# Moving small per-query work from VectorE to GpSimd and ScalarE in a differential-attention and mixture-of-experts kernel

## The chip, the cores and the metric

One NeuronCore of a Trainium2 chip runs the whole kernel. The metric is the device time of one execution in microseconds (us); the figure given for a kernel is the median of several runs. A profile is one further execution, recorded by the hardware profiler. The engines are TensorE (PE; its weight loads are PEld), VectorE (DVE), ScalarE (ACT), GpSimd (POOL) and SyncE (SP), which here only starts transfers.

## The reference

`x` is 8 x 512 x 128 in float32; there are 16 heads of width 8 and 8 experts with a hidden width of 512. Two layers follow each other, each with a residual and a layer norm:

```python
def attn(x, Wq, Wk1, Wk2, Wv, Wo, lambda_logit):
    q, k1, k2, v = heads(x @ Wq.T), heads(x @ Wk1.T), heads(x @ Wk2.T), heads(x @ Wv.T)
    a1 = softmax(causal(q @ k1.T * SCALE)); a2 = softmax(causal(q @ k2.T * SCALE))
    a = a1 - sigmoid(lambda_logit) * a2
    a = a / maximum(sum(abs(a)), 1e-6)
    return merge(a @ v) @ Wo.T

def ffn(x, gamma, beta, router_w, W1, W2):
    xn = layernorm(x) * gamma + beta
    p = softmax(xn @ router_w.T / 1.5)
    w, idx = top_k(p, 2)
    y_e = silu(xn @ W1[e]) @ W2[e]
    return sum_over_e(dense(w, idx)[e] * y_e) + x

x = layernorm(x + attn(x)); x = layernorm(x + ffn(x))
```

## The kernel before

**Attention.** For each of the 8 batches the 512 queries are cut into 16 strips of 32. A strip `j` with its keys is one `Unit`; it sees `L = 32 (j + 1)` keys. The 16 heads are 4 groups (`g`) of 4 heads, so one group's scores for a strip are 128 rows (4 heads x 32 queries) by `L` columns. A unit with `L` up to 256 ("early") is done in two slots, a longer one ("late") in four; a slot makes the scores of two groups (early: both softmaxes at once; late: one of the two). That makes 48 slots a batch and 384 in all.

Per slot: PE writes scores into one of two PSUM tiles `sc` (L327, L336); DVE takes the negated row maxima `nm` (L349, L357); ACT takes the exponentials into `et` and, through an accumulator that a second instruction reads, their row sums (L367). Per unit: DVE works out the ratio `c2` = sigmoid(lambda) * sum1 / sum2 in three tiny instructions (`ratios`, L379, L382, L383). Per piece of a unit (two groups when early, one when late), `combine`: DVE forms max(c2 * e2, e1) and its row sum (L393, which gives the absolute sum later on), POOL scales e2 by -c2 in place (L403) and may gather left-over columns into `rest` (L417), PE then transposes both tiles into one PSUM accumulation, which is also the subtraction (L448), ACT copies the result to `aT` (L473), and PE multiplies by the values (L490).

**Order.** Nothing is left to a scheduler. `round_of`, called once a slot, issues the instructions of all engines in the order in which they stand: values times, scores of the next slot, `aT` copies, `on_act`, maxima of this slot, transposes, `on_dve`, combining of pieces of the unit before, exponentials of this slot, `on_dve_late`, and then one step each of the filler work. Each engine works through its own list in that order, so an instruction that waits holds everything behind it on its engine.

**Filler work.** `misc` holds the small steps after a block of four strips (`block_tasks`: normalise, project out, residual and layer norm, turn `xnT`, L595, router logits) and the projections of the next batch (`projection_tasks`: `xT`, L251; `qs`, L268; `kT`, L276; `vt`, L284). `routing` holds the top-2 routing of a chunk of 6 or 9 blocks. `moves` are the indirect transfers that sort rows by expert into `xs`, `gathers` those that fetch results back (`got`, L925) for mixing (`mix`, L935) and the last layer norm (its root on POOL by a power, L90). `experts` holds the expert tiles of a chunk, 128 rows each: `load` (weights and `xg`, on SP), `turn` and `hidden`. `turn(t)` transposes `xg[t]` (L871) and, into the other half of the same PSUM tile `pa`, multiplies the tile three steps back by its second matrix (L880); `xgT` is made by DVE (L874), `ysb` by ACT (L890). `hidden(t)` multiplies by the first matrix into a PSUM tile `pz` (L900) of the same two-buffer pool; ACT takes the tanh (L845), DVE finishes the SiLU `hT` (L847). Experts are taken from their list at a pace that `times` and `go` set. The last sparse chunk (19 tiles) and one dense chunk (2 blocks) come after the last slot: in the tail there is no attention to hide behind.

## Time and profile before

| | before |
|---|---|
| median of 3 runs | 1220.2 us (1216.79 to 1223.67) |
| the profiled execution | 1212.04 us |
| span of its profile, first to last instruction | 1210.1 us |
| granted PE clock, mean | 0.927 |
| PE, DVE, ACT, POOL busy | 90%, 77%, 64%, 44% of the span |

The span is divided at the first maxima of a unit. By these, attention runs from about 19 us to 1087 us, and the tail takes the last 123 us. The costliest groups are the transposes (L448, PE, 326.7 us), the exponentials (L367, ACT, 300.4 us late and 188.6 us early), the scaling (L403, POOL, 270.9 us), the combining (L393, DVE, 258.6 us), and the maxima (L357, DVE, 252.0 us). A group's row in the profile gives its busy time, the mean of one instruction, and the idle time of its engine just before it with what ended that idle time. PE's busy time has modelled ends and can hold short stalls.

### The profile page before, as it was taken

Reading aid. Unit: us, or ns where it says so; the run is one execution under the profiler, and the core shown is the slowest. Engines: PE = TensorE matmul, PEld = TensorE weight load, DVE = VectorE, ACT = ScalarE, POOL = GpSimd, SP = SyncE. Lnnn points to the kernel's source line nnn. Section 1 sums busy time; section 2 is a strip of 40 time slices with the busy share of each in tenths; the row PEclk is TensorE's granted clock in tenths of the full one; section 3 lists DMA queues with packets and bytes.
Section 4 is the critical chain, followed back from the end, with each engine's and each line's share of the span. In section 5 each row is a group of like instructions: output and inputs, shape, how many; then the busy total and the mean of one; then the engine's idle time right before and its main releaser. Section 6 shows DMA issues by size and latency. Waiting matters only on the chain.

```text
span 1210.1 us, 28192 instructions
## 1 busy us (share of the span) xinstructions
PE 1093.9 (90%) x9450; PEld 776.2 (64%) x9450; DVE 927.1 (77%) x2837; ACT 780.4 (64%) x2775; POOL 526.8 (44%) x935
## 2 busy tenths in 40 slices
PE   5999899989999899989998999988999989997686
PEld 3566565555666566666666666666667667777675
DVE  4688778777887887987887878887767898874556
ACT  3678767576777777766766867774567566662221
POOL 4343433463423442267464432333554652444333
PEclk7699969797999999989998999997899799998998
DMA  4400000110221112100322222221213344444762
GB/s 133 122 8 1 10 2 8 31 56 30 50 63 46 54 32 67 45 27 27 93 69 58 73 54 68 64 73 31 81 52 91 95 120 124 122 123 129 207 177 67
DMA packets 128895, 84.28 MB, mean 70 GB/s; under 512 B 22896, under 2 KB 114288, under 8 KB 128752
## 3 DMA queue, kind: packets, MB, share of 16 engines
q1 hardware_dynamic: 111952, 68.26, 20.2%
q0 software_dynamic: 3840, 7.87, 2.3%
q10 hardware_dynamic: 12960, 6.36, 1.8%
q8 instruction: 75, 1.23, 0.4%
q14 instruction: 68, 0.56, 0.2%
HBM read 63.31 MB, written 17.56 MB: 67 GB/s over the span
## 4 chain that ended last, share of the span: by engine, by line
PE 60%; DVE 16%; ACT 11%; issue 6%; POOL 4%; DMA 3%; ACTq 1%; POOLq 0%; SPq 0%; DVEq 0%
PE pt L448 19%; PE sc L327 13%; ACT et L367 7%; PE po L490 5%; PE pz L900 5%; PE pa L880 5%; PE sc_None L327 5%; DVE junk L393 2%; DVE nm L357 2%; PE pmo L541 2%; ACT aT L473 2%; DVE nm L349 2%; POOL et L403 1%; DVE hT L847 1%; POOL xs L777 1%
## 5 line engine op out<-in xcount | busy, mean ns | idle before, releaser
L403 POOL TENSOR_SCALAR et<-et,c 128x224 f32<-128x224 f32 (+15 forms) x512 | 270.9, 534 | 458.1 <-DVE junk L393 295.0
L448 PE MATMUL pt<-ident,et 128*128 128x128 f32 (+1 forms) x2048 | 326.7, 296 | 26.8 <-ACT aT L473 14.9
L448 PEld LDWEIGHTS pt<-ident,et 128*128 128x128 f32 (+1 forms) x2048 | 230.5, 145 | 159.6 <-issue 58.2
L367 ACT ACTIVATE et<-sc,nm 128x512 f32<-128x512 f32 (+7 forms) x512 | 300.4, 595 | 48.7 <-DVE nm L357 27.6
L357 DVE TENSOR_REDUCE nm<-sc 128x2 f32<-128x576 f32 (+7 forms) x256 | 252.0, 984 | 45.1 <-PE sc L336 44.6
L473 ACT COPY aT<-pt 128x384 f32<-128x384 f32 (+5 forms) x488 | 186.1, 407 | 134.5 <-PE pt L448 130.7
L393 DVE SCALAR_TENSOR_TENSOR junk<-et,c 128x224 f32<-128x224 f32 (+15 forms) x512 | 258.6, 505 | 9.6
L327 PE MATMUL sc<-kT,qb 32*128 32x384 f32 (+7 forms) x1024 | 246.8, 559 | 10.9 <-ACT et L367 9.6
L367 ACT ACTIVATE et<-sc_None,nm 128x256 f32<-128x256 f32 (+7 forms) x512 | 188.6, 387 | 32.0 <-DVE nm L349 22.0
L327 PE MATMUL sc_None<-kT,qb 32*128 32x512 f32 (+7 forms) x512 | 116.5, 535 | 21.8 <-ACT et L367 21.0
L900 PE MATMUL pz<-xgT,w 128*128 128x128 f32 x704 | 102.1, 291 | 18.8 <-DVE xgT L874 18.5
L349 DVE TENSOR_REDUCE nm<-sc_None 128x4 f32<-128x256 f32 (+7 forms) x128 | 96.1, 751 | 29.6 <-PE sc_None L336 29.3
L327 PEld LDWEIGHTS sc<-kT,qb 32*128 32x128 f32 x1024 | 78.3, 187 | 61.3 <-ACT et L367 27.4
L367 ACT ACTIVATION_READ_ACCUMULATOR et<-sc_None,nm 128x1 f32 x512 | 108.1, 211 | 0.0
L900 PEld LDWEIGHTS pz<-xgT,w 128*128 128x128 f32 x704 | 92.5, 204 | 23.6 <-DVE xgT L874 21.2
L367 ACT ACTIVATION_READ_ACCUMULATOR et<-sc,nm 128x1 f32 x512 | 103.9, 203 | 0.0
L880 PE MATMUL pa<-w,hT 128*128 128x128 f32 x704 | 98.1, 285 | 0.6 <-ACT ysb L890 0.6
L845 ACT ACTIVATE th<-pz 128x512 f32<-128x512 f32 x88 | 52.7, 599 | 68.9 <-PE pz L900 47.9
L880 PEld LDWEIGHTS pa<-w,hT 128*128 128x128 f32 x704 | 90.9, 202 | 1.3 <-ACT ysb L890 0.7
L777 POOL DMA_INDIRECT xs<-xh,row x60 | 65.9, 1099 | 46.9 <-DMA xs<-xh,row 31.3
L490 PE MATMUL po<-aT,vt 128*32 128x128 f32 (+1 forms) x2048 | 85.3, 290 | 0.0
L847 DVE SCALAR_TENSOR_TENSOR hT<-th,pz 128x512 f32<-128x512 f32 x88 | 60.2, 684 | 30.8 <-ACT th L845 30.6
(150 smaller groups left out, 1281.0 us busy)
## 6 DMA issues: line engine op xcount, KB each, us to landing
w<-in_w_dram SPq DMA_DIRECT2D x192, 256.0 KB
xg<-xs SPq DMA_DIRECT2D x88, 64.0 KB
ys<-ysb ACTq DMA_DIRECT2D x88, 64.0 KB
xs<-zero SPq DMA_DIRECT2D x2, 1600.0 KB
xs<-zero SPq DMA_DIRECT2D x2, 1216.0 KB
xt<-in_x_dram SPq DMA_DIRECT2D x8, 256.0 KB
out_dram<-ot SPq DMA_DIRECT2D x32, 64.0 KB
vr<-vt SPq DMA_DIRECT2D x32, 32.0 KB
```

The source lines that it names most:

```text
L327: nc.tensor.matmul(parts[gi][:, :, :L], lhsT=qb[r, j].rearrange("p h q -> p (h q)"), rhs=kT[r, sets, :L], start=True, stop=False,)
L349: nc.vector.tensor_reduce(self.nm[:, g, :], sc.rearrange("p g (s l) -> p g s l", s=2)[:, :, :, : self.L], AX.X, ALU.max, negate=True,)
L357: nc.vector.tensor_reduce(self.nm[:, g, s], sc[:, :, : self.L], AX.X, ALU.max, negate=True)
L367: nc.scalar.activation(self.et[:, g, si, : self.L], sc[:, gi, lo : lo + self.L], AF.Exp, bias=self.nm[:, g, si : si + 1], accum_out=self.b ...
L393: nc.vector.scalar_tensor_tensor(junk[:, :L], self.et[:, g, 1, :L], self.c2[:, g : g + 1], self.et[:, g, 0, :L], ALU.mult, ALU.max, accum_ ...
L403: nc.gpsimd.tensor_scalar(self.et[:, g, 1, :L], self.et[:, g, 1, :L], self.c2[:, g : g + 1], -1.0, ALU.mult, ALU.mult,)
L448: nc.tensor.matmul(pt[: len(gs) * kw, x_, :], lhsT=lhsT, rhs=ident, is_transpose=True, start=(k == 0), stop=(k == 1),)
L473: nc.scalar.copy(self.aT[: rows[done], self.used + done : self.used + end, :], pt[: rows[done], done:end, :],)
L490: nc.tensor.matmul(self.blk["po"][32 * g : 32 * g + 32, self.jj, :], lhsT=v[:rows, kb, 32 * g : 32 * g + 32], rhs=self.aT[:rows, self.at[g ...
L777: nc.gpsimd.indirect_dma_start(ch.xs[:, :], bass.IndirectOffsetOnAxis(ap=ch.row[:, k, c : c + 1], axis=0), ch.xh[:, c, :], None,)
L880: nc.tensor.matmul(pm[:, 1, :], lhsT=hT[y][:, f, :], rhs=w[y][1][:, f, :], start=(f == 0), stop=(f == NF - 1),)
L900: nc.tensor.matmul(pz[:, f, :], lhsT=w[t][0][:, f * P : (f + 1) * P], rhs=xgT[t], start=True, stop=True,)
```

## The change

It has six parts.

1. The evacuations of `xT`, `qs`, `vt`, `xnT` and `xgT` go from DVE to ACT (the last two as an Identity activation with scale and bias).
2. `weighted`, issued at the end of a unit's last slot, makes c1 on POOL; for late units it makes the whole of `c2` there, with a power of -1 in place of the reciprocal.
3. For units with `L` up to 96, the maximum is taken over both groups of a piece in one instruction and summed by a second, from the already scaled e2, on `on_dve_late`.
4. A routing step goes ahead of `misc`; the two joined pairs of routing steps become single steps; the projections get a list of their own, behind `misc`.
5. In the tail `pz` takes its PSUM tile from the pool of the scores.
6. `w1st`, `w2nd` and `row` go to a pool with three buffers; a constant in `times` goes from 24 to 22.

The place of `run(on_dve_late)`, after combining and exponentials, is the same in both kernels.

```diff
+    mone = const.tile([P, NG], F32, name="mone")
+    nc.gpsimd.memset(mone, -1.0)
...
-                on_dve.append(lambda: nc.vector.tensor_copy(xT, pm))
+                on_act.append(lambda: nc.scalar.copy(xT, pm))
...
-                    nc.vector.tensor_copy(qs, pm)
+                    nc.scalar.copy(qs, pm)
...
-                    nc.vector.tensor_copy(vt, pm)
+                    nc.scalar.copy(vt, pm)
...
             def ratios(self):
                 sums, jj = self.blk["sums"], self.jj
-                c1 = sp.tile([P, NG], F32, tag="c1", name=f"c1_{self.b}_{self.j}")
-                nc.vector.tensor_mul(c1, sums[:, 0, jj, :], slam)
+                if self.c2 is not None:
+                    return
                 self.c2 = sp.tile([P, NG], F32, tag="c2", name=f"c2_{self.b}_{self.j}")
                 r2 = sp.tile([P, NG], F32, tag="r2", name=f"r2_{self.b}_{self.j}")
                 nc.vector.reciprocal(r2, sums[:, 1, jj, :])
-                nc.vector.tensor_mul(self.c2, c1, r2)
+                nc.vector.tensor_mul(self.c2, self.c1, r2)
+
+            def weighted(self):
+                self.c1 = sp.tile([P, NG], F32, tag="c1", name=f"c1_{self.b}_{self.j}")
+                nc.gpsimd.tensor_tensor(self.c1, self.blk["sums"][:, 0, self.jj, :], slam, ALU.mult)
+                if not self.early:
+                    self.c2 = sp.tile([P, NG], F32, tag="c2", name=f"c2_{self.b}_{self.j}")
+                    nc.gpsimd.tensor_tensor(
+                        self.c2, self.blk["sums"][:, 1, self.jj, :], mone, ALU.pow
+                    )
+                    nc.gpsimd.tensor_tensor(self.c2, self.c1, self.c2, ALU.mult)
...
-                L = self.L
-                for g in piece:
-                    nc.vector.scalar_tensor_tensor(
-                        junk[:, :L],
-                        self.et[:, g, 1, :L],
-                        self.c2[:, g : g + 1],
-                        self.et[:, g, 0, :L],
-                        ALU.mult,
-                        ALU.max,
-                        accum_out=self.blk["big"][:, self.jj, g : g + 1],
-                    )
+                L, g0, m = self.L, piece[0], len(piece)
+                small = L <= 96
+
+                def largest():
+                    first, second = (self.et[:, g0 : g0 + m, k, :L] for k in range(2))
+                    big = self.blk["big"][:, self.jj]
+                    if small:
+
+                        both = junk[:, : m * L].rearrange("p (g l) -> p g l", g=m)
+                        nc.vector.scalar_tensor_tensor(both, second, -1.0, first, ALU.mult, ALU.max)
+                        nc.vector.tensor_reduce(big[:, g0 : g0 + m], both, AX.X, ALU.add)
+                        return
+                    for k, g in enumerate(piece):
+                        nc.vector.scalar_tensor_tensor(
+                            junk[:, :L],
+                            second[:, k],
+                            self.c2[:, g : g + 1],
+                            first[:, k],
+                            ALU.mult,
+                            ALU.max,
+                            accum_out=big[:, g : g + 1],
+                        )
+
+                if not small:
+                    largest()
                 for g in piece:
                     nc.gpsimd.tensor_scalar(
...
+                if small:
+                    on_dve_late.append(largest)
...
-                on_dve.append(
-                    lambda: nc.vector.tensor_scalar(s["xnT"], pm, gam, bet, ALU.mult, ALU.add)
+                on_act.append(
+                    lambda: nc.scalar.activation(
+                        s["xnT"], pm, AF.Identity, bias=bet, scale=gam
+                    )
                 )
...
-            tasks = [largest, first, second, together(weights, chosen), counts]
-            tasks += [together(starts, rows), owners]
+            tasks = [largest, first, second, weights, chosen, counts]
+            tasks += [starts, rows, owners]
...
-                    on_dve.append(
-                        lambda: nc.vector.tensor_scalar(
-                            xgT[t], pm[:, 0, :], gam, bet, ALU.mult, ALU.add
+                    on_act.append(
+                        lambda: nc.scalar.activation(
+                            xgT[t], pm[:, 0, :], AF.Identity, bias=bet, scale=gam
                         )
                     )
...
-                pz = ps_m.tile([P, NF, P], F32, tag="pm", name=f"pz_{n0}_{t}")
+
+                pool, tag = (ps_s, "sc") if attention_done else (ps_m, "pm")
+                pz = pool.tile([P, NF, P], F32, tag=tag, name=f"pz_{n0}_{t}")
...
-                behind = seq * (24 + (2 * ch.nb + 3 if ch.sparse else 0)) / 48
+                behind = seq * (22 + (2 * ch.nb + 3 if ch.sparse else 0)) / 48
...
-            if misc:
-                misc.popleft()()
-                room -= 1
+
             if routing:
                 step = routing.popleft()
                 step()
                 room -= step.__name__ == "counts"
+            elif misc or proj:
+                (misc or proj).popleft()()
+                room -= 1
+            if now and now["left"] == 1:
+                now["u"].weighted()
...
-                        misc.extend(projection_tasks(b + 1))
+                        proj.extend(projection_tasks(b + 1))
```

## The prediction, made before the changed kernel was run

> **What bounds the kernel now.** I read the busy shares and the 40 slices, then the stages, the waits of PE, one turn of the tail in order of time, and the clock.
>
> ```profile
> PE 1093.9 (90%) x9450; PEld 776.2 (64%) x9450; DVE 927.1 (77%) x2837; ACT 780.4 (64%) x2775; POOL 526.8 (44%) x935
> ...
> PE   5999899989999899989998999988999989997686
> ```
>
> PE is the bound nearly throughout, with 116 us idle in a span of 1210.1; no work leaves it in this change. So the question is which of its waits go, and which come. The stage view, summed first over the eight early halves of a batch (strips 0 to 7), then over the eight late halves, then the tail:
>
> ```profile
> sum 385.89, PE 341.00 PEld 233.51 DVE 300.84 ACT 269.18 POOL 190.51; mean PE 42.63 PEld 29.19 DVE 37.60 ACT 33.65 POOL 23.81
> ...
> sum 681.84, PE 656.47 PEld 458.35 DVE 552.14 ACT 478.24 POOL 282.46; mean PE 82.06 PEld 57.29 DVE 69.02 ACT 59.78 POOL 35.31
> ...
> 1086.70:1166.50 79.80, 56.69 (x452) 51.53 (x452) 42.41 (x137) 21.95 (x52) 28.45 (x34) 0.91 0.59 165
> ```
>
> Late halves leave PE 25.4 us idle out of 681.8, early ones 44.9 out of 385.9, the sparse part of the tail 23.1 out of 79.8. PE's waits between 50 and 1087 us come to some 63 us; the largest (us in total, times, longest):
>
> ```profile
> PE sc_None L327 <- ACT et L367: 17.1, 31, 1.1
> PE pt L448 <- ACT aT L473: 11.9, 23, 0.7
> PE pt L448 <- POOL et L403: 9.7, 17, 1.6
> PE sc L327 <- ACT et L367: 9.6, 23, 0.8
> PE pa L871 <- DVE hT L847: 5.0, 4, 2.1
> ```
>
> ACT stands in front of PE for 38.6 us, POOL for 9.7, DVE mostly behind these: in the same stretch ACT waited 43.7 us for the maxima (L357 and L349), and POOL's scaling 277.0 us for the combining. One turn of the tail:
>
> ```profile
> 1128.55 1.16 PE L900 MATMUL pz<-xgT,w 128*128 128x128 f32 x8 [0.80 <-DVE xgT L874]
> ...
> 1129.65 1.06 PE L880 MATMUL pa<-w,hT 128*128 128x128 f32 x8
> ...
> 1130.74 0.27 ACT L890 COPY ysb<-pa 128x128 f32<-128x128 f32 x1 [0.41 <-PE pa L880]
> ...
> 1131.04 0.41 DVE L874 TENSOR_SCALAR xgT<-pa,gam,bet 128x128 f32<-128x128 f32 x1 [1.04 <-ACT ysb L890]
> ```
>
> `xgT` starts only 0.03 us after `ysb` has ended, though its data were there when the transpose ended at 1129.8. It does so all along: DVE stood idle 45.8 us in front of L874 for `ysb`, 40.3 of it during attention.
>
> The clock, either side of 627.4 us (the numbers after the busy times are clock, DMA share and GB/s):
>
> ```profile
> 620.60:624.00 3.40, 3.33 (x27) 2.33 (x23) 3.09 (x16) 2.38 (x6) 2.40 (x3) 1.00 0.07 19
> 624.00:627.40 3.40, 1.31 (x10) 1.08 (x11) 3.40 (x8) 1.76 (x5) 2.59 (x4) 1.00 0.14 41
> 627.40:630.80 3.40, 3.40 (x42) 2.69 (x42) 3.06 (x10) 1.57 (x5) 1.83 (x4) 0.50 0.77 212
> ```
>
> A stretch in which PE was 39% busy is followed by one at half clock. Over the eight batches from 30 us on, the granted clock was 0.88, 0.86, 0.93, 1.00, 0.95, 0.97, 0.91 and 0.96: times their lengths, 69 us of full clock are missing.
>
> **The change, part by part.** The sum is made against the profiled execution, 1212.0 us (a span of 1210.1 with 1.9 around it), which is 8.2 below the median of 1220.2.
>
> *Evacuations to ACT.* DVE loses 88 `xgT` (0.407 each, 35.8), 32 `xnT` (12.9) and 24 copies (16.5). ACT gains them. An Identity with two pointers isn't in the trace: from below the plain ACT copy of that size (0.27), from above the exponential of 128x128 (0.37); I take 0.32. With 24 copies at 0.59 (`kT`) that is 52.6 us more on ACT, some 44 of it during attention. In ACT's order `xgT` now stands in front of `ysb`; both wait for the L880 products. Were there a table load for each function change, it would cost 1.28 us (the one in the trace); the changed program has a single load, as before.
> In the tail the ring of 2.96 us loses `ysb` and its hand-over (0.30) and 0.09 of `xgT`: 0.39 on 9 turns, 3.5 us. While results are gathered (turns of 3.4 to 3.8 us from 1136 on) the ring runs DVE `mix`, POOL's power, DVE `ot`, `xgT`, `hT`; it loses the 0.40 of `xgT` on 7 turns, 2.8 us. `pz` in the scores' pool means that the next product waits for `hT` two tiles back and not one, which lets that happen. Sum -6.3; bounds 0 (if weights, at 576 KB a turn, arrive no faster) and -15.9, all that PE waited for `xgT` there.
> In attention the DVE stalls of 40.3 us go. Of PE's waits I count `xgT` itself (2.9), half of L871's on `hT` and of L448's on POOL (7.4) and a quarter of the 26.7 on exponentials: -17. Bounds 0 and -44 (all of these).
> More work on ACT: 44 on 747 us busy is 6%; PE's 38.6 us behind ACT grow in proportion, +2.3; bounds 0 and +12 (a quarter of what is added).
>
> *Late ratios on POOL.* DVE loses 128 c1 (22.4) and 64 reciprocals and products (22.3). On POOL a power takes 0.574 for one column and 0.704 for two (medians), so four at the same step 0.96; between 0.70 and 1.25. A product of 128x4 isn't in the trace: the 128x8 memset (0.11) below, the 128x32 scaling (0.29) above; I take 0.2. POOL then has 100 us more and is 52% busy. c1 hides behind the last exponentials; the ratio is ready 1.2 us after them (0.9 to 1.6).
> Before, the first combining of a late unit began in the median 1.5 us after the last exponential, in 31 of 64 units under 1.2. Without its own three instructions (0.47) DVE would come earlier: set against 1.2, 31 units combine later, 14.4 us in all, 33 earlier, 15.2 in all. Behind the waiting combining stand the next maxima, behind `weighted` on POOL the sends, gathers and powers of that slot; what is late next is the scaling, then the transposes, a slot later. PE waited for scaling in 17 places only; a quarter of 14.4 gets through, +3.6; bounds 0 and +27.0 (ratio at 1.6, all gets through).
> The Trainium skill (GPSIMD Engine Reference, section 4.1 Engine selection) speaks against this: two-input elementwise work belongs on VectorE, GpSimd being about twice as slow. By that the product would be twice DVE's 0.175, the ratio ready at about 1.35 and the later starts some 19 us. No row here has a product on POOL to try it on.
>
> *Short units (24, two pieces each).* POOL scales 0.45 to 0.50 earlier, as it no longer follows the combining. DVE pays as much as before (two of 0.25 to 0.32 plus a read of 0.08 each, against one of twice the length, 0.29 to 0.42, and a reduction of 0.2 to 0.4), but holds for the two scalings: 0.6 to 0.7 on 48 pieces, 33 us, with the next maxima behind it. The cover is DVE's 22% idle in early halves, and its loss of c1. Taken +4; bounds -8 (a third of the earlier scaling) and +17 (half of 33).
>
> *Routing first, projections last, more buffers, 22 for 24.* In the order of PE the 175 expert products behind the last score are the same, and the rest shift by a slot or two. `vt` and the eight `vr` transfers on SP come some five slots later; the next batch needs them 20 slots on (14 in one batch). Weights queue behind them on SP, which is already far ahead (350 us waiting for buffers). 0; without that cover, about a slot of 2.5 us a batch, 17.
>
> *Clock.* PE's waits in attention fall by 17 less 9.9, a ninth. If half-clock time falls in proportion, and half of the 69 is felt, -4; bounds -35 and +17.
> The Trainium skill (TensorE: Matmul & The Clock Gate, section HAM oscillation) asks for a PE gap of over about 3.4 us before the clock falls. By that no short wait here would matter, and this term would be 0. The rows at 624 us differ: PE was still 39% busy there, its longest wait 1.3 us.
>
> Sum: -6.3 - 17 + 2.3 + 3.6 + 4 + 0 - 4 = -17.4, 1212.0 to 1194.6; against the median, **1202.8, say 1203**.
>
> **The rivals.**
> - *VectorE stands still for GpSimd (slower).* The ratio comes at 1.6 us and all of it gets through: +27.0, +17 for short units, against -6.3 and -17: +20.7, 1241. It decides from the point where PE's waits for the scaling grow by more than the 23 us gained. For it: POOL is in order, and 31 units have no slack. Against: a slot of spare time lies between scaling and transposes, and PE waited there only 9.7 us.
> - *PE is full anyway.* Late halves are 96% busy; only the tail gains, and the costs eat the rest: -6.3 + 2.3 + 3.6 = 1220. For it: DVE is named in 8.5 us of PE's waits only. Against: DVE stands behind both ACT and POOL.
> - *The clock holds.* PE's waits halve (-31), and with them the missing clock, half of it felt (-17), with -6.3: 1166 at best, half-way to it from the forecast 1184. For it: falls of the clock follow short waits in early strips. Against: they come in batches 1, 4 and 6, not in 3, under the same code.
> - *It doesn't do what it says.* The combining of short units, left over to `on_dve_late`, stands behind combining as before, not in front; that is the +17 above and needs no case of its own.
>
> **How the numbers follow.** Forecast 0.50, its own range 1192 to 1214; clock 0.12; full anyway 0.12; slower 0.26. The range reaches most of the way to both ends: 1182 to 1237. About 0.5%, 6 us, can't be told from no change. Faster: 0.47 of the forecast, 0.12, 0.03, makes 0.62; within: 0.03 and 0.07, 0.10; slower: 0.26 and 0.02, 0.28.
>
> **What would show it.** Right: no wait of `xgT` for `ysb`; tail turns of 2.6 us without gathering and some 3.4 with it; PE's waits for exponentials under 22 us; a clock above 0.93. Wrong: DVE idle before L416 for POOL with more than 20 us, or PE waiting for the scaling more than 20 us; a power of over 1.25 us; ACT's copies `aT` in front of PE for 20 us.

## The result: slower by 3.1%, and the profile after

| | before | after |
|---|---|---|
| median of 6 runs each | 1218.82 us | 1260.32 us |
| ratio, with its 95% interval | | 1.0307 (1.0241 to 1.0373) |
| the profiled execution | 1212.04 us | 1246.92 us |
| its span | 1210.1 us | 1245.2 us |
| granted PE clock, mean | 0.927 | 0.916 |

Ratios here are taken over undisturbed runs of both kernels and can differ from the ratio of two medians. The profiled execution is the fastest of the six, so the profile shows 35 us of the loss.

Lines move in the new code. Exponentials are L369, maxima L351 and L359, combining L416 (short units L412 and L413), scaling L429, transposes L476, `aT` L501; `c1` on POOL is L389, the power L392, the product L395; `xgT` is L897 and `pz` L925.

Busy time of PE, its slices, and the clock:

```profile
PE 1109.5 (89%) x9450; PEld 783.7 (63%) x9450; DVE 852.0 (68%) x2341; ACT 831.3 (67%) x2919; POOL 640.7 (51%) x1192
...
PE   5989899988999899988999899998889888998785
...
PEclk8699877797899999987999899997899999998998
```

VectorE lost 75 us of work and POOL gained 114. PE has the same 9450 matmuls and is busy 15.6 us longer, which fits the clock: over the whole span half-clock time rose by 32 us (178.8 to 210.9). The stage view says where (the sum over the early halves, strips 0 to 7, of the eight batches; the sum over the late halves; the tail):

```profile
sum 404.48, PE 354.12 PEld 241.94 DVE 278.30 ACT 276.11 POOL 206.32; mean PE 44.27 PEld 30.24 DVE 34.79 ACT 34.51 POOL 25.79
...
sum 708.70, PE 662.52 PEld 460.62 DVE 507.67 ACT 513.56 POOL 378.56; mean PE 82.81 PEld 57.58 DVE 63.46 ACT 64.19 POOL 47.32
...
1130.27:1245.20 114.93, 85.27 (x643) 77.13 (x642) 61.65 (x182) 37.31 (x81) 46.54 (x57) 0.92 0.59 169
```

Early halves took 18.6 us longer, late halves 26.9, and the tail 8.5 less (it was 123.4). In attention PE's busy time grew by 13.1 + 6.1 = 19.2 and its idle time by 5.5 + 20.8 = 26.3: about 45 us, part new waits and part a slower clock on the same work. Half-clock time between 50 us and the end of attention rose from 116 us in 11 stretches to 157 in 17.

PE's waits in that part (us in total, times, longest):

```profile
PE sc L329 <- ACT et L369: 19.7, 29, 3.5
PE sc_None L329 <- ACT et L369: 19.4, 31, 2.2
PE pt L476 <- POOL et L429: 15.9, 24, 2.6
PE pt L476 <- ACT aT L501: 11.5, 20, 0.9
PE pmr L554 <- POOL rexp L549: 11.2, 13, 1.4
PE pmn L617 <- DVE xh L604: 5.8, 5, 1.4
```

Waits for exponentials went from 26.7 to 39.1 us, for the scaling from 9.7 to 15.9, for `rexp` from 3.5 to 11.2. These three are behind ACT and POOL, which in turn wait for VectorE; which part of the change makes which of them, the experiments show. VectorE's own waits in the same part:

```profile
DVE nm L359 <- PE sc L338: 89.2, 99, 2.9
DVE junk L416 <- POOL c L395: 71.8, 52, 3.4
...
DVE hT L870 <- ACT th L868: 28.0, 29, 3.9
DVE junk L412 <- POOL et L429: 20.5, 22, 1.7
```

Two of these rows did not exist before: VectorE stands still 71.8 us for the ratio (one more wait, of 3.6 us, falls in the tail; of the 75.4 in all, 67.9 lie behind the last row sum) and 20.5 us for the scaling of short units. In the group rows (busy and mean ns, then idle before and its cause):

```profile
L416 DVE SCALAR_TENSOR_TENSOR junk<-et,c 128x128 f32<-128x128 f32 (+12 forms) x416 | 235.9, 567 | 83.2 <-POOL c L395 75.4
...
L925 PE MATMUL pz<-xgT,w 128*128 128x128 f32 x704 | 99.1, 286 | 0.0
...
L392 POOL TENSOR_TENSOR c<-sums,mone 128x4 f32<-128x4 f32 x64 | 65.7, 1026 | 45.5 <-ACT et L369 44.7
```

The power took 1.03 us, inside the forecast's bounds of 0.70 to 1.25. PE no longer waits for `xgT` in front of `pz` at all (18.5 us before). One place where the first row's idle time arises, in order of time:

```profile
262.38 0.64 POOL L429 TENSOR_SCALAR et<-et,c 128x448 f32<-128x448 f32 x1
...
263.08 0.40 POOL L445 COPY rest<-et 128x256 f32<-128x256 f32 x1
263.13 0.21 ACT L369 ACTIVATION_READ_ACCUMULATOR et<-sc,nm 128x1 f32 x1
263.45 0.20 POOL L389 TENSOR_TENSOR c<-sums,slam 128x4 f32<-128x4 f32 x1
...
263.61 1.04 POOL L392 TENSOR_TENSOR c<-sums,mone 128x4 f32<-128x4 f32 x1
...
264.72 0.20 POOL L395 TENSOR_TENSOR c<-c,c 128x4 f32<-128x4 f32 x1
...
264.96 0.72 DVE L416 SCALAR_TENSOR_TENSOR junk<-et,c 128x480 f32<-128x480 f32 x1 [3.43 <-POOL c L395]
...
265.08 1.58 POOL L807 DMA_INDIRECT xs<-xh,row  x1 [0.16 <-issue]
...
265.60 1.22 DVE L359 TENSOR_REDUCE nm<-sc 128x2 f32<-128x1024 f32 x1
266.72 1.18 POOL L429 TENSOR_SCALAR et<-et,c 128x480 f32<-128x480 f32 x1
...
266.86 0.69 ACT L369 ACTIVATE et<-sc,nm 128x512 f32<-128x512 f32 x1 [2.17 <-DVE nm L359]
...
267.95 1.40 PE L476 MATMUL pt<-ident,et 128*128 128x128 f32 x7 [2.56 <-POOL et L429]
```

The unit's last row sum is read by 263.34. POOL is then just ending the scaling and the copy of the unit before, so its three steps follow each other from 263.45 to 264.92: the ratio is there 1.6 us after the sums. VectorE's three steps would have taken 0.47. Behind the combining stand the next maxima (265.60) and behind them the exponentials, for which ACT has waited 2.17; on POOL a send of 1.58 stands between the product and the scaling, for which PE has waited 2.56. In this place a wait on VectorE comes out as one of ACT, for the maxima, and one of PE, for the scaling.

Over the 64 late units the ratio was ready in the median 1.39 us after the last row sum, at least 1.37 and at most 4.98; in 23 units the power began more than 0.1 us after the sums (0.08 at the least), held by POOL's own queue.

What the clock makes of such a place (length, busy times of PE, PEld, DVE, ACT and POOL, then clock, DMA share and GB/s):

```profile
260.40:263.80 3.40, 2.94 (x20) 1.79 (x19) 1.13 (x1) 2.41 (x7) 2.66 (x6) 1.00 0.09 28
263.80:267.20 3.40, 1.59 (x10) 0.56 (x8) 2.24 (x4) 0.93 (x2) 3.11 (x4) 1.00 0.00 0
267.20:270.60 3.40, 2.65 (x35) 2.19 (x39) 2.56 (x5) 2.26 (x8) 2.72 (x3) 0.67 0.12 39
...
297.80:301.20 3.40, 1.72 (x12) 0.89 (x13) 3.23 (x10) 2.16 (x11) 0.63 (x3) 0.69 0.43 139
301.20:304.60 3.40, 3.40 (x16) 2.00 (x14) 2.38 (x11) 2.90 (x16) 1.51 (x4) 0.50 0.00 0
```

PE 47% busy in one stretch, and the next is granted 0.67. At 298 us the clock falls within the stretch in which PE is 51% busy (granted 0.69), and the next is all at half clock. This second place is a short unit of 96 keys:

```profile
297.53 0.49 DVE L412 SCALAR_TENSOR_TENSOR junk<-et 128x192 f32<-128x192 f32 x1 [1.14 <-POOL et L429]
...
298.05 0.35 DVE L413 TENSOR_REDUCE big<-junk 128x2 f32<-128x192 f32 x1
298.32 0.68 DVE L351 TENSOR_REDUCE nm<-sc_None 128x4 f32<-128x512 f32 x1
...
299.04 0.37 ACT L369 ACTIVATE et<-sc_None,nm 128x128 f32<-128x128 f32 x1 [2.44 <-DVE nm L351]
```

VectorE waits 1.14 us for the scaling, combines, and only then makes the maxima for which ACT has been idle 2.44 us.

The tail did what was forecast. Two turns:

```profile
1145.42 0.47 ACT L897 ACTIVATE xgT<-pa,bet,gam 128x128 f32<-128x128 f32 x1
...
1146.62 1.06 PE L925 MATMUL pz<-xgT,w 128*128 128x128 f32 x8
...
1147.19 0.46 ACT L897 ACTIVATE xgT<-pa,bet,gam 128x128 f32<-128x128 f32 x1
...
1147.62 1.06 PE L903 MATMUL pa<-w,hT 128*128 128x128 f32 x8
...
1148.52 1.06 PE L925 MATMUL pz<-xgT,w 128*128 128x128 f32 x8
```

`xgT` of the next tile is ready before PE asks for it, and `ysb` no longer stands in front. From one `pz` to the next it is in the median 2.8 us over 18 turns, against 3.8 over 18 before.

### The profile page after: what moved, and what is told of

The parts are those of the page before. It is cut to its first block, busy times and chain, and to the rows that moved or that the text cites. A ratio compares the mean times of both kernels' runs of the same rounds, so it can differ in the third digit from the quotient of the medians.

```text
span 1245.2 us, 27911 instructions
## 1 busy us (share of the span) xinstructions
PE 1109.5 (89%) x9450; PEld 783.7 (63%) x9450; DVE 852.0 (68%) x2341; ACT 831.3 (67%) x2919; POOL 640.7 (51%) x1192
## 3 DMA queue, kind: packets, MB, share of 16 engines
q8 instruction: 76, 1.25, 0.4%
## 4 chain that ended last, share of the span: by engine, by line
PE 54%; DVE 14%; ACT 11%; POOL 8%; DMA 6%; issue 5%; ACTq 1%; SPq 0%; POOLq 0%; DVEq 0%
PE pt L476 17%; PE sc L329 11%; ACT et L369 7%; PE po L518 5%; PE sc_None L329 5%; PE pa L903 4%; PE pz L925 4%; DMA xs<-xh,row 4%; DVE junk L416 3%; PE pmo L569 2%; POOL c L392 2%; POOL et L429 2%; DVE nm L359 2%; DVE nm L351 2%; ACT aT L501 1%
## 5 line engine op out<-in xcount | busy, mean ns | idle before, releaser
L429 POOL TENSOR_SCALAR et<-et,c 128x224 f32<-128x224 f32 (+15 forms) x512 | 275.8, 546 | 304.4 <-DVE junk L416 285.2
L476 PE MATMUL pt<-ident,et 128*128 128x128 f32 (+1 forms) x2048 | 333.1, 300 | 35.0 <-POOL et L429 16.8
L476 PEld LDWEIGHTS pt<-ident,et 128*128 128x128 f32 (+1 forms) x2048 | 234.6, 147 | 169.7 <-issue 49.2
L369 ACT ACTIVATE et<-sc,nm 128x512 f32<-128x512 f32 (+7 forms) x512 | 300.6, 597 | 48.0 <-DVE nm L359 28.4
L359 DVE TENSOR_REDUCE nm<-sc 128x2 f32<-128x576 f32 (+7 forms) x256 | 252.2, 985 | 89.6 <-PE sc L338 89.2
L416 DVE SCALAR_TENSOR_TENSOR junk<-et,c 128x128 f32<-128x128 f32 (+12 forms) x416 | 235.9, 567 | 83.2 <-POOL c L395 75.4
L501 ACT COPY aT<-pt 128x384 f32<-128x384 f32 (+5 forms) x488 | 186.4, 408 | 143.1 <-PE pt L476 137.3
L369 ACT ACTIVATE et<-sc_None,nm 128x256 f32<-128x256 f32 (+7 forms) x512 | 188.7, 388 | 36.7 <-DVE nm L351 27.4
L329 PE MATMUL sc_None<-kT,qb 32*128 32x512 f32 (+7 forms) x512 | 119.5, 550 | 26.8 <-ACT et L369 25.9
L351 DVE TENSOR_REDUCE nm<-sc_None 128x4 f32<-128x256 f32 (+7 forms) x128 | 95.9, 750 | 36.3 <-PE sc_None L338 35.9
L369 ACT ACTIVATION_READ_ACCUMULATOR et<-sc_None,nm 128x1 f32 x512 | 108.9, 213 | 0.0
L369 ACT ACTIVATION_READ_ACCUMULATOR et<-sc,nm 128x1 f32 x512 | 105.0, 205 | 0.0
L925 PE MATMUL pz<-xgT,w 128*128 128x128 f32 x704 | 99.1, 286 | 0.0
L925 PEld LDWEIGHTS pz<-xgT,w 128*128 128x128 f32 x704 | 90.9, 201 | 2.2 <-issue 1.4
L392 POOL TENSOR_TENSOR c<-sums,mone 128x4 f32<-128x4 f32 x64 | 65.7, 1026 | 45.5 <-ACT et L369 44.7
L807 POOL DMA_INDIRECT xs<-xh,row x60 | 69.4, 1157 | 37.4 <-DMA xs<-xh,row 33.3
L518 PE MATMUL po<-aT,vt 128*32 128x128 f32 (+1 forms) x2048 | 88.1, 299 | 0.0
```

What stands on the lines that cost most here:

```text
L329: nc.tensor.matmul(parts[gi][:, :, :L], lhsT=qb[r, j].rearrange("p h q -> p (h q)"), rhs=kT[r, sets, :L], start=True, stop=False,)
L351: nc.vector.tensor_reduce(self.nm[:, g, :], sc.rearrange("p g (s l) -> p g s l", s=2)[:, :, :, : self.L], AX.X, ALU.max, negate=True,)
L359: nc.vector.tensor_reduce(self.nm[:, g, s], sc[:, :, : self.L], AX.X, ALU.max, negate=True)
L369: nc.scalar.activation(self.et[:, g, si, : self.L], sc[:, gi, lo : lo + self.L], AF.Exp, bias=self.nm[:, g, si : si + 1], accum_out=self.b ...
L392: nc.gpsimd.tensor_tensor(self.c2, self.blk["sums"][:, 1, self.jj, :], mone, ALU.pow)
L416: nc.vector.scalar_tensor_tensor(junk[:, :L], second[:, k], self.c2[:, g : g + 1], first[:, k], ALU.mult, ALU.max, accum_out=big[:, g : g ...
```

## The experiments

The theory: a hand-over to POOL in the middle of VectorE's order costs more than it takes off VectorE, because the maxima and the scaling stand behind it. The rivals: more work on ACT slows the exponentials; the new order starves PE; POOL is simply too full. "The evacuations" below are part 1 of the change with the buffers of part 6 and, unless said otherwise, the tail's `pz` of part 5. The buffers stand in every kernel below, so no run says what they do by themselves. Every ratio is to the kernel before, in the same comparison, with its 95% interval.

**One part undone at a time.** The first kernel makes both ratios on VectorE again:

```diff
             def ratios(self):
-                if self.c2 is not None:
-                    return
+                c1 = sp.tile([P, NG], F32, tag="c1", name=f"c1_{self.b}_{self.j}")
+                nc.vector.tensor_mul(c1, sums[:, 0, jj, :], slam)
...
-            if now and now["left"] == 1:
-                now["u"].weighted()
```

> The changed kernel with both ratios back on VectorE (three small instructions a unit, nothing on GpSimd), all else as changed. Theory S (VectorE stands still for the ratio from GpSimd, 70.9 us in attention): most of the loss goes, 1205 to 1225 us, the wait of the combining for GpSimd is gone and TensorE's waits for the scaling fall from 15.9 us to under 10. Theory A (the evacuations overload ScalarE) or theory O (the new order of the filler): still above 1240.

Measured: 1.0122 (1.0087 to 1.0157), with a median of 1230.36 us, 5 above the range that the theory gave. Of the 3.1%, 1.85 points or 22.5 us go with the ratios alone. PE's waits for the scaling fall from 15.9 to 4.1 us, as expected, and those for `rexp` from 11.2 to 1.7; its waits for the exponentials do not fall (39.1 to 43.6). VectorE's idle time in front of the combining falls from 83.2 to 7.1 us; its group row:

```profile
L416 DVE SCALAR_TENSOR_TENSOR junk<-et,c 128x128 f32<-128x128 f32 (+12 forms) x416 | 233.6, 562 | 7.1
```

The first combining now follows the last row sum by 0.90 us in the median, where the whole change had 1.43 and the kernel before 1.51. So the evacuations do bring VectorE to the combining sooner, and the ratio on POOL takes that back. In means, which hold the long waits, the three have 1.16, 1.81 and 1.67.

The second has the old short units:

```diff
-                small = L <= 96
+                small = False
```

> The changed kernel with the short units (up to 96 keys) combined as before, group by group and ahead of the scaling. Theory S counts 22.7 us of VectorE waits for the scaling, in strips that TensorE leaves partly idle: 5 to 15 us faster than the changed kernel, 1245 to 1255. Theories A and O: no change, about 1260.

Measured: 1.0154 (1.007 to 1.0238), 1.5 points or 19 us less than the change. This rests on two of the four runs, which are 16 us apart; by the medians of all runs it is 0.9 points or 11 us.

The third has the five evacuations back on VectorE:

```diff
-                on_act.append(lambda: nc.scalar.copy(xT, pm))
+                on_dve.append(lambda: nc.vector.tensor_copy(xT, pm))
...
-                        lambda: nc.scalar.activation(
-                            xgT[t], pm[:, 0, :], AF.Identity, bias=bet, scale=gam
+                        lambda: nc.vector.tensor_scalar(
+                            xgT[t], pm[:, 0, :], gam, bet, ALU.mult, ALU.add
```

> The changed kernel with all five evacuations back on VectorE. Theory S: VectorE has 65 us more to do and again stands still for the expert outputs behind the ratio from GpSimd, so slower than the changed kernel, 1262 to 1280. Theory A: faster, 1225 to 1240, with less wait of TensorE for exponentials.

Measured: 1.0331 (1.026 to 1.0402), not to be told from the change. Taking ACT's extra work away doesn't help. But it also takes away the gain of the tail, and PE's waits for the exponentials fall from 39.1 to 31.6 us, so this run alone doesn't clear ACT; the evacuations alone, below, do.

The fourth has the old filler order (joined routing steps, `misc` with the projections ahead of routing, 24 for 22):

```diff
+            if misc:
+                misc.popleft()()
+                room -= 1
             if routing:
...
-            elif misc or proj:
-                (misc or proj).popleft()()
-                room -= 1
```

> The changed kernel with the old order of the filler (misc ahead of routing, joined routing steps, projections in misc, 24 in the pace). Theory O: faster by 15 us or more, under 1245. Theories S and A: within 6 us of the changed kernel, 1254 to 1266.

Measured: 1.0226 (1.018 to 1.0272), 0.8 points less, with overlapping intervals.

**The evacuations alone** (the kernel before with these and nothing else):

> Of the change only the evacuations on ScalarE, the tail's pool and the buffers are left; ratios, short units and the order of the filler are as before. Theory S+O (VectorE held by GpSimd, and starved steps of a block, cost all of the loss): the forecast's gains come out, 1200 to 1212 us, faster than before by 0.5 to 1.5%, with the tail near 115 us. Theory A (ScalarE's load costs too): 1217 to 1235, no faster than before.

Measured: 0.9878 (0.9783 to 0.9973). So ACT's load is not what makes the change slow. The tail takes 11.7 us less; from the first to the last maxima the profile has 1070 us against 1066. VectorE has 37 us less to do there and ACT 42 more. ACT's waits for the maxima fall from 43.7 to 27.8 us, but PE's for the exponentials rise from 26.7 to 33.9, and all of PE's waits together go from 63.4 to 66.1: PE gains nothing there that can be told. This kernel is known to about one point either way, and so is every distance to it below; three kernels whose totals can't be told from it (`pz` in its old pool, the idle ratio on POOL, the new order) stand at 0.9827 to 0.9886.

**POOL's part doubled.** The power is made twice, the second time for nothing:

```diff
+                    nc.gpsimd.tensor_tensor(
+                        self.c2, self.blk["sums"][:, 1, self.jj, :], mone, ALU.pow
+                    )
                     nc.gpsimd.tensor_tensor(self.c2, self.c1, self.c2, ALU.mult)
```

> The changed kernel with the power of the late ratio done twice on GpSimd, some 1.02 us later in each of 64 late units (65 us more on GpSimd). Theory S: VectorE's wait for the ratio grows from 71 us to 110 or more and the time by 20 to 45 us, to 1280 to 1305. Rival (the ratio's wait is absorbed by the slot of spare time before the transposes, and the loss lies elsewhere): within 8 us of the changed kernel.

Measured: a median of 1345.6 us (1325.94 to 1352.75), where the kernel before had 1213.72. 64 units times 1.02 us are 65 us of POOL; the time rose by 85 over the change's median, nearly twice the most that the theory gave. The rows, with lines three further on:

```profile
L479 PE MATMUL pt<-ident,et 128*128 128x128 f32 (+1 forms) x2048 | 354.4, 311 | 55.3 <-POOL et L432 39.7
...
L419 DVE SCALAR_TENSOR_TENSOR junk<-et,c 128x128 f32<-128x128 f32 (+12 forms) x416 | 236.6, 569 | 144.7 <-POOL c L398 136.7
```

VectorE's wait grew by 61 us, about as much as was added. PE felt less of it as idle time: between the two profiles attention grew by 97 us, PE's idle time in it by 27, most of that waits for the scaling (15.9 to 37.7). Half-clock time grew from 157 to about 318 us, worth up to 80 us of full clock, with a mean clock of 0.863. What is added on this hand-over comes through whole on VectorE, and on PE mostly through the clock.

**POOL busy, but nobody waits.** To tell the hand-over from POOL's occupancy, VectorE makes and uses the late ratio, and POOL makes it too, at a result that nothing reads (its last product is the power with itself), on top of the evacuations:

```diff
-                self.c1 = sp.tile([P, NG], F32, tag="c1", name=f"c1_{self.b}_{self.j}")
+                self.c1 = sp.tile([P, NG], F32, tag="c1p", name=f"c1p_{self.b}_{self.j}")
...
+            if now and now["left"] == 1 and not now["u"].early:
+                now["u"].weighted()
```

> The evacuations alone, with the late ratios on VectorE and used from there, and beside them the same three instructions on GpSimd in the same place, whose result nobody uses. Theory S in its narrow form (only VectorE's standing still for the ratio costs): as the evacuations alone, 1196 to 1209 us. Rival Q (GpSimd held in its own order by the wait for ScalarE, and 78 us busier, so that scaling, sends and roots come late): as with the late ratios on GpSimd, 1215 to 1235.

Measured: 0.9883 (0.9812 to 0.9953), as without it. POOL's 91 us more of work, and what stands behind them there, cost nothing that can be told; by the two intervals some 0.7 points can't be excluded.

**The late ratio on POOL, and used**, with the evacuations and nothing else:

```diff
+                if self.c2 is not None:
+                    return
...
+            if now and now["left"] == 1 and not now["u"].early:
+                now["u"].weighted()
```

> The evacuations alone plus the late ratios on GpSimd (early ones wholly on VectorE). Theory S: this one part costs most of the distance from evacuations alone to the whole change (some 52 us): 1225 to 1245 us, with 60 us or more of VectorE waits for the ratio and half-clock time well above 116 us. Rival (the parts cost only together): 1200 to 1212.

Measured: 1.0113 (1.0058 to 1.0168). Against the evacuations alone that is 2.35 points or 28.6 us. It and the run before it have the same work on POOL, and only the use differs (there the three steps are issued ahead of the filler, here behind it; they end 1.52 and 1.40 us after the sums in the median). Their intervals are apart, so most of the price is the wait for the ratio and not POOL's work.

VectorE's wait, and PE's for the scaling, here and (last row) with the evacuations alone:

```profile
DVE junk L418 <- POOL c L397: 66.8, 51, 4.3
PE pt L478 <- POOL et L431: 21.2, 25, 2.6
...
PE pt L476 <- POOL et L429: 10.1, 15, 1.8
```

PE waits 11 us more for the scaling, and for the exponentials as before (33.3 and 33.9), though ACT's own waits for the maxima grew from 27.8 to 44.5. So the late ratio reaches PE through combining and scaling: the mirror image of the first experiment. Half-clock time came to 126 us, not "well above 116"; but this profile is of the fastest of the six runs, 11 us under their median.

**Only the first product on POOL**, for all units, reciprocal and second product on VectorE:

```diff
-                if not self.early:
-                    self.c2 = sp.tile([P, NG], F32, tag="c2", name=f"c2_{self.b}_{self.j}")
-                    nc.gpsimd.tensor_tensor(
-                        self.c2, self.blk["sums"][:, 1, self.jj, :], mone, ALU.pow
-                    )
-                    nc.gpsimd.tensor_tensor(self.c2, self.c1, self.c2, ALU.mult)
```

> The evacuations alone, with only the first product of each ratio (0.2 us) on GpSimd for all 128 units; reciprocal and second product stay on VectorE. Theory S: the product needs only the first sums and is mostly ready in time, so at most 8 us slower than the evacuations alone, 1196 to 1212. Rival (any hand-over from GpSimd in front of the combining costs, by its place behind the scaling in GpSimd's order): 1213 to 1225.

Measured: 0.9784 (0.9719 to 0.9848), better than both kernels; the distance to the evacuations alone, 0.9 points, is within the intervals. `c1` needs only the sums of the first softmax, which a late unit has a slot before its last one, so the product can run before the ratio is wanted, and VectorE waits for it seldom:

```profile
DVE c L385 <- POOL c L389: 15.6, 14, 2.4
```

A hand-over to POOL isn't dear in itself; one that is mostly on time is cheap.

**Short units.** The evacuations with the new short units:

```diff
-                small = False
+                small = L <= 96
```

> The evacuations alone plus the new combining of short units. Theory S: 5 to 15 us slower than the evacuations alone, 1204 to 1215. Rival (short units cost nothing by themselves, only when VectorE is also late for the ratio): within 4 us of the evacuations alone.

Measured: 1.0023 (0.9987 to 1.0058), 1.45 points or 17.6 us over the evacuations alone. Among the waits of VectorE and, in attention, of PE are two of the change's new rows:

```profile
DVE junk L412 <- POOL et L429: 24.7, 28, 1.5
...
PE pmn L617 <- DVE xh L604: 5.9, 5, 1.5
```

On PE it isn't the exponentials (32.8 us against 33.9 with the evacuations alone) that wait longer. In the second row PE waits for a block's layer norm `xh`, which VectorE now finishes late. The change has this row too (5.8 us), and the kernel with the evacuations alone hasn't.

Then the same, but with the two VectorE instructions a slot later, when POOL has scaled:

```diff
-                    on_dve_late.append(largest)
+                    on_dve_next.append(largest)
...
             run(on_dve)
+            run(on_dve_next)
```

> The evacuations alone plus the new combining of short units, but with VectorE's two instructions of a piece a slot later, ahead of that slot's combining, by when the scaling is done; nothing else moves. Theory S (what the short units cost is VectorE standing still for the scaling, with the next maxima behind it): as the evacuations alone, 1195 to 1209 us. Rival (the wide instruction with its separate sum costs as such): as the short units before, 1214 to 1226.

Measured: 0.9782 (0.9736 to 0.9828), with 1186.91 us the lowest median of all, though its ratio can't be told from 0.9784. The first row shrinks to

```profile
DVE junk L412 <- POOL et L429: 0.9, 2, 0.6
```

and the second is gone. So the new combining of short units is no worse than the old one; its place in VectorE's order cost 2.4 points, some 29 us.

In the whole change the left-over steps were put ahead of combining:

```diff
             run(on_dve)
+            run(on_dve_late)
...
-            run(on_dve_late)
             room = 2
```

> The changed kernel with the left-over VectorE steps run ahead of combining: the maxima of short units come a slot later, when their scaling is done, and the SiLU goes ahead of the combining. Theory S: VectorE's 22.7 us of waits for the scaling fall under 8, and the time by as much as taking the short units back did, 5 to 15 us, to 1245 to 1255. Rival (short units cost through their extra instructions or not at all): no change, 1254 to 1266.

Measured: 1.0289 (1.0193 to 1.0384), no gain that can be told. The wait of L412 is gone here too (0.2 us), but other steps are in the same list: `hT` now comes before its tanh is ready, and VectorE's wait for that rose from 28.0 to 61.5 us. A wait was moved, not removed.

**Order.** The evacuations with the new order:

> The evacuations alone plus the new order of the filler (routing first, single steps, projections last, 22). Theory O: 8 to 20 us slower than the evacuations alone, 1207 to 1220. Rival (the order costs nothing once nothing else is late): within 4 us.

Measured: 0.9886 (0.9841 to 0.993), as without it. The whole change with both a routing step and a filler step in a slot:

```diff
-            elif misc or proj:
+            if misc or proj:
```

> The changed kernel, but a slot takes a step of routing and one of misc or the projections, so that routing no longer holds up the steps of a block; single routing steps, the projections' own list and the 22 stay. Theory O as starvation (ScalarE stood 3.3 us before oraw for a block's late step on VectorE): as the old order did, 8 to 20 us faster than the changed kernel, 1240 to 1252, without the waits of oraw for the product L559. Rival (another part of the new order, such as the single steps): no change, 1254 to 1266.

Measured: 1.0372 (1.0276 to 1.0468), no gain. PE's longest wait for exponentials fell from 3.5 to 1.7 us, so the long waits at late block steps are not likely to be the cost. Last, what hadn't been found guilty: evacuations, first product on POOL, new order:

> The whole change without its two costly parts: late ratios' power and second product back on VectorE, short units as before; evacuations, first products on GpSimd, new order of the filler and the tail's pool stay. Theory S: as the evacuations with the first products, 1190 to 1205, faster than both kernels. Theory O: the new order costs 8 us or more on top, 1203 to 1215.

Measured: 0.9915 (0.987 to 0.996), 1.3 points or 16 us over the same without the new order, with intervals apart.

**The evacuations taken apart.** Tail `pz` back in its old pool:

```diff
-                pool, tag = (ps_s, "sc") if attention_done else (ps_m, "pm")
+                pool, tag = ps_m, "pm"
```

> The evacuations alone with the expert tiles of the tail back in the pool that they shared with the turned rows. Forecast's view (the tail gains by both): 2 to 6 us slower, 1201 to 1206, tail turns without gathering near 3 us. Rival (the pool matters not, the gain of the tail is all xgT's): within 2 us.

Measured: 0.9827 (0.9772 to 0.9882). That pool brings nothing that can be told by the total; in the profiles the tail takes 111.7 us with it and 115.3 without, inside the 2 to 6 us of the forecast's view. The kernel before with `xgT` alone on ACT:

> The kernel before, with nothing changed but xgT on ScalarE. View T (the gain of the evacuations is the tail's ring, and xgT makes it): 8 to 15 us faster than before, 1202 to 1211. View D (VectorE's relief through all five evacuations makes it): 2 to 5 us faster.

Measured: 0.9905 (0.9869 to 0.9941). And with the other four and not `xgT`:

> The kernel before with the other four evacuations (xT, qs, vt, xnT) on ScalarE and xgT left on VectorE. View T: no change, 1213 to 1222. View D: faster by 6 us or more, under 1211.

Measured: 0.9951 (0.9915 to 0.9987). By these two about two thirds of the gain is `xgT`; their intervals overlap. In the profiles the tail takes 9.9 us less with `xgT` alone and 3.2 less with the other four.

**Where each cost falls.** Time by strips, summed over the eight batches, one profile each (us, worked out from the starts of the units' first maxima; the last strip of the last batch is left out):

| strips | 0-1 | 2-5 | 6-8 | 9-12 | 13-15 |
|---|---|---|---|---|---|
| before | 97 | 165 | 215 | 308 | 269 |
| evacuations alone | 97 | 163 | 210 | 316 | 273 |
| with late ratios | 113 | 166 | 199 | 325 | 272 |
| with short units | 98 | 189 | 202 | 313 | 271 |
| with short units, a slot later | 98 | 162 | 208 | 318 | 268 |
| with first product on POOL | 100 | 164 | 201 | 315 | 272 |
| the same and new order | 95 | 171 | 196 | 342 | 261 |
| whole change | 105 | 184 | 199 | 347 | 265 |

The three costs lie apart. The late ratio costs most in strips 0 and 1, where strip 15 of the batch before is combined. Short units cost in strips 2 to 5, and not when moved a slot. The new order costs 27 us in strips 9 to 12 and 7 in strips 2 to 5, and gives 22 back elsewhere; on the evacuations alone it costs 26 in strips 9 to 12 (316 to 342) and gives 22 back. The next batch's `vt` is made in strip 9 without it and in strips 10 to 13 with it, and PE's waits for the exponentials in strips 9 to 12 go from 6.7 to 17.0 us. That this is the way the order costs is a reading of profiles; no run moved the projections alone. The whole change has all three.

In each place PE's idle time grows by little and half-clock time by much (us, from the evacuations alone to the kernel with that one part, one profile each):

| part, strips | length | PE idle | half clock |
|---|---|---|---|
| late ratios, 0-1 | 97 to 113 | 19.8 to 24.8 | 10 to 36 |
| short units, 2-5 | 163 to 189 | 14.9 to 20.5 | 47 to 101 |
| new order, 9-12 | 316 to 342 | 12.3 to 23.0 | 17 to 52 |

At half clock at most half of the time is lost, so new idle time and that half together make 18, 33 and 28 us, where 16, 26 and 26 were measured. In these strips five to eleven us of new stalls thus went with two to five times as much time. Over the whole of attention the late ratio adds 11 us of PE's idle time and 10 of half-clock time, as other strips have less of it. Half-clock time in one place differs from profile to profile (in strips 2 to 5, 43 to 65 us in twelve of the thirteen kernels that do without the new combining or move it, 84 in the other, and 72 to 115 in the seven that have it), so the sizes are rough.

## Why the prediction was wrong

The forecast was 1203 us, with a range to 1237; it came to 1260. Term by term:

- *Tail, -6.3.* Right: -8.5 in the profile of the change. The step from `ysb` to `xgT` was the mechanism, as PE's wait of 0.0 shows; the other pool for `pz` adds 3.6 us by the profiles and nothing that the totals show.
- *VectorE's relief in attention, -17.* Wrong. 37 us less VectorE work left attention as long as before (1070 against 1066 us). Its lower bound of 0 came nearest: ACT got the maxima sooner, but PE did not get the exponentials sooner. That the work added to ACT ate up the gain fits the waits and was not tested apart.
- *More work on ACT, +2.3, at most +12.* Too small by PE's waits for the exponentials: 7 us more with the evacuations alone (26.7 to 33.9), 7.5 less when they are taken out of the change. In the total it isn't separable from the relief; undoing both gains nothing. The Identity took 0.46 us where 0.32 was taken.
- *Late ratios, +3.6, at most +27.* This is the step that failed most: 22.5 us out of the change, 28.6 on top of the evacuations. The price of the power (0.96 taken, 1.03 measured) and of the product (0.2, and 0.203) were right. Too small was "ready 1.2 us after them (0.9 to 1.6)", which left out that `weighted` queues on POOL behind scaling, copy and sends (1.39 in the median, 1.74 in the mean, up to 4.98). Wrong was the start that it was set against: the kernel before's 1.5 us, though the evacuations bring VectorE to the combining at 0.90. Against the kernel before, 39 units combine later, 33.6 us in all, and 25 earlier, 24.1 (forecast 14.4 and 15.2); against the change without the ratio on POOL, 53 units combine later, 46.6 us in all. And wrong was "a quarter of 14.4 gets through": the spare slot between scaling and transposes, on which I built, did not protect the transposes. PE waits 11 to 12 us more for the scaling with the late ratio than without it (10.1 to 21.2, and 4.1 to 15.9), most of it in strips 0 and 1 and 9 to 12. In strips 0 and 1 half clock then stands in all seven later batches, against two of the seven with the evacuations alone. Why the combining of the isolated kernel, which in the median starts no later than that of the kernel before (1.44 against 1.51), makes PE wait 11 us longer for the scaling stays open.
- *Short units, +4, at most +17.* The mechanism was in the text ("holds for the two scalings") and the size wasn't: 17.6 us on the evacuations, its upper bound, and 11 to 19 out of the change. The cover of 22% idle VectorE in early halves is no cover for what stands right behind the wait, the maxima and, as PE's waits show, `xh`.
- *Order, 0, without cover 17.* Some 16 us in one pair (0.9784 to 0.9915), 10 in another with overlapping intervals, none that can be told in the third, whose profile shows the same shift between the strips. The likely place is strips 9 to 12. How the three add isn't settled.
- *Clock, -4.* Wrong in sign: from 0.927 to 0.916, as PE's waits grew. In the strips where the three costs fall, the table above makes it the larger part of each.

The slower rival named the mechanism, VectorE standing still for GpSimd, and its sign: the warning level of 20 us of idle time before L416 was passed with 75.4. Its path, PE's waits for the scaling, is the one that the experiments show for the late ratio, but not at its size: alone these waits grew by 11 us, in the change by 6, short of the 23 at which it was to decide; and its 1241 priced no loss of clock. The 12 us more that PE waits for the exponentials in the change belong to other parts: 7 come with the evacuations, and the new order adds 12 to these (33.9 to 45.5), the late ratio none; the two don't simply add in the whole change. The 8 us more for `rexp` go when the ratio goes (11.2 to 1.7), but the late ratio alone has only 3.4; they need other parts as well. "PE is full anyway" is not what happened: PE has 26 us more idle time in attention. "It doesn't do what it says" was true of the left-over step and belongs to the +17.

Against the kernel before, the parts come in points to -1.2 for the evacuations, -0.9 for the first product (overlapping intervals), +2.35 for late ratios, +1.45 for short units and +0.8 for the order: +2.4, where the whole is +3.1 (2.4 to 3.7). The first product stands in two of these, its own and the late ratios.

By the page GPSIMD Engine Reference of the Trainium skill, section 4.1 Engine selection, two-input elementwise work is about twice as slow on GpSimd. The rows here differ for four columns: 203 ns for the product on POOL and 169 to 178 on VectorE, a factor of 1.2. The slow step is the power, 1026 ns against VectorE's reciprocal of 170. The page's choice, VectorE for such work, is right here for the late ratio; the first product cost nothing on GpSimd.

By the page TensorE: Matmul & The Clock Gate of the Trainium skill, section HAM oscillation, idle gaps of over about 3.4 us are to be kept out. The rows at 263.8 and 297.8 us differ: half clock followed the first stretch and set in within the second, in which PE was 47% and 51% busy, and PE's longest gaps just before were 2.56 and 1.24 us.

## What to carry to other kernels

Before a small step goes to another engine, look not at its length but at who waits for the result, in order, and what stands behind the waiting instruction: here 1.4 us on an engine with time to spare held VectorE, and VectorE held the scaling that PE waits for. Hand over only what is ready a slot before it is used (the first product, and the short units' maxima a slot later, cost nothing on top of the evacuations), and put a consumer where its input is sure to be there. A busy engine that is off the path gave nothing that could be told here when it was relieved, so price relief by what the bounding engine waits for, and set a hand-over against the start that the rest of the change allows. Then look which of the bounding engine's waits grew in the isolated run: in the whole change the waits of three parts stand in the same rows.

Two versions beat both kernels: the evacuations with the first product on POOL (0.9784), and the evacuations with short units combined a slot later (0.9782). The two together were not tried.

## What the hardware showed that was not expected

- The price of a stall was more than its length, through the clock: 65 us added to the hand-over made 85 us, with half-clock time going from 157 to about 318 while PE's idle time grew by 27. In the strips where the isolated parts cost, 5 to 11 us of new idle time stood beside 26 to 54 us more at half clock.
- The price of a power on POOL grows with the columns: 0.57 us for one, 0.70 for two, 1.03 for four (the forecast's 0.96 was taken from the first two). A product is 0.2 us there for four.
- An Identity with scale and bias read from pointers, 128x128 out of PSUM, takes ACT 0.46 us, above both bounds given for it (0.27 for a copy, 0.37 for an exponential), and 0.05 more than VectorE took.
